# One piece of expert work to each scan, instead of 0.85, beside the last chunk of a Mamba and mixture-of-experts kernel

## The chip, the cores and the metric

The kernel runs on one core of a Trainium2 chip. The metric is device time in microseconds (us) of one execution. Before the change it is 1593.14 us, the median of three runs (1592.46 to 1595.06). The profile comes from one further execution, which took 1591.91 us, with 1590.2 us between its first and its last instruction.

The five engines are named as in the profile: PE (matrix multiply, with its weight loads as PEld), DVE (vector), ACT (activation), POOL (general), SP (issues DMAs). Each runs its own instructions in a fixed order and waits on semaphores for the others.

## The reference, cut to what matters

A layer over 4 sequences of 1024 tokens of 256 channels: a selective-scan (Mamba) block, a layer norm, a mixture of experts with a shared expert, and a second layer norm.

```python
# Mamba block, N = 16 states, 512 inner channels
deltaA  = exp(delta[..., None] * A)
deltaBx = (delta * xs)[..., None] * B[:, :, None, :]
ys      = associative_scan(a*x + b, over time)          # per channel and state
y       = einsum('blcn,bln->blc', ys, C)
x1      = layernorm(x + x + ((y + xs * D) * silu(res)) @ w_out)

# experts: 8, the best 2 of each token, hidden size 1024, and one shared
normed  = rmsnorm(x1)
comb    = top-2 of sigmoid(normed @ router.T), normalised
moe     = shared(normed) + sum over e of comb[:, e] * (relu(normed @ ew1[e] + eb1) @ ew2[e] + eb2)
out     = layernorm(x1 + moe)
```

## The kernel before, in words

The 4096 tokens are cut into 8 chunks of 512, two to a sequence, handled in order. I number them 0 to 7; `chunks[-1]` is chunk 7.

**The scans.** For each chunk the main loop (L1084 on) goes over the 16 states n, and in each over the KB = 4 blocks of 128 channels: 64 scans to a chunk. One scan is an exponential on ACT (`da`, L513) and a scan on DVE (`hs`, L516), 1.21 to 1.27 us each. Once per state DVE also makes the next state's inputs (`hs` from `xs`, L444) and multiplies by C (L529), and POOL adds to `y` (L530). The rows B and C that these take are spread over the partitions by a small matmul on PE (`pb`, L430), issued some scans ahead; its PSUM tiles share a pool of three with other tiles.

**What is put beside the scans.** The work around the scans is written as Python generators, which the main loop steps: `front` (projections, convolution, softplus of the next chunk), `tail` (output projection, layer norm, router and dispatch of the chunk before), and `moe` (the experts). Beside chunk 7 there is no `front`, as no chunk follows; the tail of chunk 6 is stepped once per scan there, through the list `ending`.

**The experts' work.** `moe()` (L975) works through 100 units of 128 token rows: for each chunk 4 units of the shared expert, whose rows are ready when the tail has made `x1T` and `combT`, and then 3, 9, 8, 8, 8, 8, 8 and 16 units of routed rows, which are gathered once the tail has scattered its rows to DRAM (`scatter`, L701) and made its plan. A unit is `up` (32 matmul records, two halves, `pu`, L900; then ReLU on ACT into `h`, L909) and `down` (16 records, two halves, `pd`, L929). Each half ends in a `yield`, so a unit is **four pieces**. The weights of a routed unit, 1 MB for up and 1 MB for down, are fetched per unit on SP's queue into two buffers each. A routed unit ends with an accumulating indirect DMA on POOL (L962); two shared units together end with an accumulating DMA on POOL (L950) out of the single buffer `rs`, which ACT fills (L945).

**How many pieces.** `other_work(share)` (L1079) adds `at_once * share` to an account, `at_once` being 0.85 and the share 1 for these chunks, and takes one piece from `moe` for each whole unit in it. If nothing is ready, `moe` yields False and the account is set to zero. After the last scan the loop `while ending` steps the tail of chunk 7, with one piece after each of its steps; what is left of `moe` follows, and then `finish` reads the sums back, normalises and writes out.

The order in which the code emits work is a priority, not the engines' order: the builder may bring an instruction forward on its engine if its inputs are thought to be ready earlier.

Of the kernel before, what the change touches and what calls it, by code (L numbers as in the profile page):

```python
# [24 lines left out]
LEN, FIRST = {}, {}  # L25
# [3 lines left out]
MAXC = max(LEN.values())  # L29
# [41 lines left out]
def mamba_moe_kernel(  # L71
# [32 lines left out]
    def load_x(b, c):  # L104
        first, n = FIRST[b, c], LEN[b, c]
        t = two.tile([P, n // P, D], F32, tag="x", name=f"x_{b}_{c}", bufs=3)
        nc.sync.dma_start(t, x[b, first : first + n, :].rearrange("(t p) d -> p t d", p=P))
        return t
# [142 lines left out]
    chunks = list(LEN)  # L251
# [173 lines left out]
    def over_partitions(step, row):  # L425

        b, c, n = step
        TC = LEN[b, c]
        pb = ps_mix.tile([P, TC], F32, tag="mix", name=f"pb_{b}_{c}_{row}")
        nc.tensor.matmul(  # L430
            pb, lhsT=pick[:, row : row + 1].to_broadcast([P, P]), rhs=scans[b, c][3],
            start=True, stop=True,
        )
        return pb

    def inputs(step, pb):
        b, c, n = step
        xs, TC = scans[b, c][0], LEN[b, c]

        on_pool = KB - 2 if (b, c) == chunks[0] else KB - 1  # L440
        copy = two.tile([P, TC], F32, tag="b", name=f"b_{b}_{c}_{n}")
        nc.scalar.copy(copy, pb)  # L442
        hs = wide.tile([P, KB, TC], F32, tag="s", name=f"hs_{b}_{c}_{n}")
        nc.vector.tensor_tensor(  # L444
            hs[:, 0:on_pool, :], xs[:, 0:on_pool, :],
            pb.unsqueeze(1).to_broadcast([P, on_pool, TC]), ALU.mult,
        )
        for k in range(on_pool, KB):
            nc.gpsimd.tensor_tensor(hs[:, k, :], xs[:, k, :], copy, ALU.mult)  # L449
        return hs  # L450
# [26 lines left out]
    def diagonal(step):  # L477

        n, TT = step[2], LEN[chunks[0]] // P
        d = two.tile([P, TT, P], F32, tag="w1", name=f"diagonal_{n}")  # L480
        shape = [P, TT, P]
        nc.gpsimd.tensor_tensor(
            d, ident.unsqueeze(1).to_broadcast(shape),
            by_token[1][:, :, n : n + 1].to_broadcast(shape), ALU.mult,
        )
        return d

    def products(step, d):

        n, TT = step[2], LEN[chunks[0]] // P  # L490
        for k in range(KB):
            pool, tag = (ps_dn, "dn") if (n * KB + k) % 3 == 2 else (ps_up, "up")
            pu = pool.tile([P, TT, P], F32, tag=tag, name=f"in_{n}_{k}")
            for t in range(TT):
                nc.tensor.matmul(
                    pu[:, t, :], lhsT=by_token[0][:, t, k * P : (k + 1) * P], rhs=d[:, t, :],
                    start=True, stop=True,
                )
            scaled_inputs.append(pu.rearrange("p t j -> p (t j)"))
            yield  # L500

    def by_pe(step):
        return step[0:2] == chunks[0] and step[2] >= 3

    def scan(step, hs, of):
        b, c, n = step
        delta, TC = scans[b, c][1], LEN[b, c]
        for k in of:
            if by_pe(step):
                da = hid.tile([P, TC], F32, tag="h", name=f"da_{b}_{c}_{n}_{k}")  # L510
            else:
                da = ps_da.tile([P, TC], F32, tag="da", name=f"da_{b}_{c}_{n}_{k}")
            nc.scalar.activation(  # L513
                da, delta[:, k, :], AF.Exp, scale=chan_sb[:, k, CA + n : CA + n + 1]
            )
            nc.vector.tensor_tensor_scan(  # L516
                hs[:, k, :], da, scaled_inputs.pop(0) if by_pe(step) else hs[:, k, :], 0.0 if c == 0 else state[:, k, n : n + 1],
                ALU.mult, ALU.add,
            )

    def keep(step, hs):
        b, c, n = step
        if c + 1 < len(CHUNKS[b]):
            nc.scalar.copy(state[:, :, n : n + 1], hs[:, :, LEN[b, c] - 1 : LEN[b, c]])

    def outputs(step, hs, pb):
        b, c, n = step
        y = scans[b, c][2]
        nc.vector.tensor_tensor(hs, hs, pb.unsqueeze(1).to_broadcast([P, KB, LEN[b, c]]), ALU.mult)  # L529
        nc.gpsimd.tensor_tensor(y, y, hs, ALU.add)  # L530
# [524 lines left out]
    order = [(b, c, n) for b, c in chunks for n in range(N)]  # L1055

    beside, ending, work = [], [], moe()
    at_once = 0.85

    def advance(count):  # L1060
        for _ in range(count):
            if not next(work, False):
                return False
        return True

    def side(of):
        for g in list(of):
            if next(g, "end") == "end":
                of.remove(g)
# [3 lines left out]
    def other_work(share):  # L1073
        nonlocal owed
        owed += at_once * share
        while owed >= 1.0:
            owed = owed - 1.0 if advance(1) else 0.0
# [10 lines left out]
    for i, step in enumerate(order):  # L1088
        b, c, n = step
        place = chunks.index((b, c))  # L1090
        more = i + 1 < len(order)
        for k in range(KB):
            if k == 0 and more and n + 1 < N:
                if by_pe(order[i + 1]):
                    over_b = diagonal(order[i + 1])
                else:
                    over_b = over_partitions(order[i + 1], n + 1)
            if k == KB // 2 and more and by_pe(order[i + 1]):
                coming = products(order[i + 1], over_b)
            next(coming, None)  # L1100
            if k == KB // 2:
                over_c = over_partitions(step, N + n)
                if more and n + 1 == N:
                    over_b = over_partitions(order[i + 1], 0)
            scan(step, hs, [k])
            if k == 0 and late is not None:
                keep(*late[0:2])
            if k == KB // 2 - 1:
                if late is not None:
                    outputs(*late)  # L1110
                    if n == 0:
                        list_of = ending if place + 1 == len(chunks) else beside
                        list_of.append(tail(*chunks[place - 1]))
                if n == 0 and place + 1 < len(chunks):
                    beside.append(front(*chunks[place + 1]))
                if n == 3:
                    beside.append(scans[b, c][4]())
                if n == N // 2 and place + 2 < len(chunks):
                    xs_in[chunks[place + 2]] = load_x(*chunks[place + 2])
                side(beside)  # L1120
            if k == KB - 1:
                late = (step, hs, over_c)
                if more and by_pe(order[i + 1]):
                    hs = wide.tile([P, KB, LEN[b, c]], F32, tag="s", name=f"hs_{b}_{c}_{n + 1}")
                elif more:
                    hs = inputs(order[i + 1], over_b)
                side(beside)
            side(ending)
            other_work(LEN[b, c] / MAXC)
    keep(*late[0:2])  # L1130
    outputs(*late)
    ending.append(tail(*chunks[-1]))
# [73 lines left out]
```

## Time and profile before

| what | value |
|---|---|
| median of three runs | 1593.14 us |
| profiled execution | 1591.91 us, span 1590.2 us |
| chunk 7's scans, first start to last end | 1201.5 to 1358.7 us |
| last sum into `y` of chunk 7 ends (POOL) | 1366.0 us |
| output projection of chunk 7 (`po`) starts on PE | 1366.79 us |
| router of chunk 7 (`pr`) starts on PE | 1392.51 us |
| first routed rows of chunk 7 are transposed on PE | 1423.68 us |
| last expert matmul ends | about 1551 us |
| reading the sums back, layer norm, output | from 1556 us to the end |

Busy time over the span is 1279.8 us on DVE, 1254.7 on PE, 1141.6 on POOL and 1065.6 on ACT. All times in the profile count from the first instruction. A row of a group gives the line in the code, the engine, the operation, the tiles written and read, and the busy time; a row of waits gives who waited for whom, for how long in total, how often, and the longest.

### The profile page before, as it was taken

How to read it: one execution, taken by the hardware profiler on the slowest of the kernel's cores; microseconds unless marked ns; L12 is line 12 of the kernel's file. 1: busy time of each engine (PE TensorE's matmuls, PEld its weight loads, DVE VectorE, ACT ScalarE, POOL GpSimd, SP SyncE). 2: the span in 40 equal slices, each digit the busy share in tenths (PEclk: the TensorE clock that was granted, in tenths of full speed). 3: DMA queues.
4: the chain of work that ended last, by engine and by line, in shares of the span. 5: the costliest groups of instructions: out<-in, count | busy, mean ns of one | idle time of the engine just before them, and what ended most of it. 6: DMA issues, size and time to landing. Idle time of an engine off the chain costs nothing. (4 is left out here: it accounts for less than half of the span.)

```text
span 1590.2 us, 20804 instructions
## 1 busy us (share of the span) xinstructions
PE 1254.7 (79%) x6639; PEld 970.3 (61%) x6639; DVE 1279.8 (80%) x1422; ACT 1065.6 (67%) x2345; POOL 1141.6 (72%) x886
## 2 busy tenths in 40 slices
PE   5588467865688788879798889888879889899990
PEld 2356324652356666677567756776667768789990
DVE  3999899989997898999998999899989899320005
ACT  5757458764778578877788778766886666434442
POOL 2468975798578876998789978997699887431223
PEclk8699678987788999999999999899899999999995
DMA  4000000440016562475236633563166538659996
GB/s 121 1 0 1 26 14 17 146 119 17 13 61 192 173 182 64 147 220 168 50 124 204 190 80 122 159 197 107 35 209 185 153 116 249 177 153 323 315 273 217
DMA packets 160275, 211.64 MB, mean 133 GB/s; under 512 B 20617, under 2 KB 138130, under 8 KB 160162
## 3 DMA queue, kind: packets, MB, share of 16 engines
q1 hardware_dynamic: 135954, 181.75, 35.2%
q0 software_dynamic: 17216, 21.57, 7.6%
q10 hardware_dynamic: 6992, 6.95, 1.3%
q8 instruction: 54, 0.88, 0.2%
q14 instruction: 59, 0.48, 0.1%
HBM read 178.97 MB, written 31.27 MB: 132 GB/s over the span
## 5 line engine op out<-in xcount | busy, mean ns | idle before, releaser
L530 POOL TENSOR_TENSOR y<-y,hs 128x2048 f32<-128x2048 f32 x128 | 597.1, 4665 | 81.2 <-DVE hs L529 80.8
L513 ACT ACTIVATE da<-delta,chan_sb 128x512 f32<-128x512 f32 x512 | 353.0, 697 | 193.1 <-DVE hs L516 190.6
L929 PE MATMUL pd<-w,h 128*128 128x256 f32 x1600 | 386.7, 386 | 22.5 <-ACT h L909 11.5
L929 PEld LDWEIGHTS pd<-w,h 128*128 128x128 f32 x1600 | 298.8, 193 | 92.8 <-issue 20.5
L516 DVE TENSOR_TENSOR_SCAN hs<-da,state,hs 128x512 f32<-128x512 f32 x256 | 317.8, 1270 | 27.1 <-ACT da L513 26.0
L900 PEld LDWEIGHTS pu<-xT,w 128*128 128x128 f32 x2176 | 276.6, 204 | 64.7 <-ACT xT L883 45.5
L900 PE MATMUL pu<-xT,w 128*128 128x128 f32 x2176 | 281.3, 288 | 28.0 <-ACT xT L883 28.0
L529 DVE TENSOR_TENSOR hs<-hs,pb 128x2048 f32<-128x2048 f32 x128 | 290.7, 2271 | 3.3 <-PE pb L430 1.6
L909 ACT ACTIVATE h<-pu,wb 128x128 f32<-128x128 f32 x800 | 229.3, 368 | 71.9 <-PE pu L900 67.2
L516 DVE TENSOR_TENSOR_SCAN hs<-da,hs 128x512 f32<-128x512 f32 x204 | 240.9, 1209 | 21.2 <-ACT da L513 20.7
L449 POOL TENSOR_TENSOR hs<-xs,b 128x512 f32<-128x512 f32 x118 | 170.6, 1448 | 67.9 <-ACT b L442 48.9
L444 DVE TENSOR_TENSOR hs<-xs,pb 128x1536 f32<-128x1536 f32 (+1 forms) x115 | 197.9, 1722 | 13.2 <-ACT b L442 7.5
L962 POOL DMA_INDIRECT sums<-rb,xb x68 | 108.0, 1588 | 131.3 <-ACT xT L883 43.8
L293 PE MATMUL pi<-hT,w_in_sb 128*128 128x512 f32 x256 | 143.0, 683 | 32.6 <-DVE xs L325 12.3
L430 PE MATMUL pb<-parts,pick 128*128 128x512 bf16 x243 | 98.2, 407 | 77.1 <-DVE hs L529 27.6
L900 PEld LDWEIGHTS pu<-x1T,w 128*128 128x128 f32 x1024 | 130.9, 203 | 13.8 <-issue 10.0
L900 PE MATMUL pu<-x1T,w 128*128 128x128 f32 x1024 | 136.4, 290 | 0.0
L219 DVE BATCH_NORM_STATS2 bnst_l<-o 128x6 f32<-128x256 f32 x32 | 11.9, 411 | 153.9 <-DMA o<-sums 153.9
L293 PEld LDWEIGHTS pi<-hT,w_in_sb 128*128 128x128 f32 x256 | 49.9, 213 | 97.3 <-issue 34.2
L562 PE MATMUL po<-w_out_sb,y 128*128 128x256 f32 x256 | 70.0, 435 | 36.6 <-POOL y L552 29.1
L562 PEld LDWEIGHTS po<-w_out_sb,y 128*128 128x128 f32 x256 | 55.5, 222 | 56.3 <-POOL y L552 36.3
L705 POOL DMA_INDIRECT rows<-hn,to x64 | 63.4, 990 | 32.1 <-issue 15.8
(198 smaller groups left out, 1555.8 us busy)
## 6 DMA issues: line engine op xcount, KB each, us to landing
w<-in_ew SPq DMA_DIRECT2D x136, 1024.0 KB, 5.7
w<-in_sw SPq DMA_DIRECT2D x16, 1024.0 KB, 5.3
xb<-rows SPq DMA_DIRECT2D x68, 129.0 KB, 5.1
x<-in_x SPq DMA_DIRECT2D x8, 512.0 KB, 4.2
sums<-summed ACTq DMA_DIRECT2D x8, 512.0 KB, 3.0
sums<-rs POOLq DMA_DIRECT2D x16, 256.0 KB, 6.6
o<-sums SPq DMA_DIRECT2D x3, 1024.0 KB, 8.8
out<-o ACTq DMA_DIRECT2D x3, 640.0 KB, 3.3
```

The lines of the kernel that those rows point to most:

```text
L293: nc.tensor.matmul(pi, lhsT=w_in_sb[:, k, m * P : (m + 1) * P], rhs=hT[:, k, :], start=(k == 0), stop=(k == KD - 1),)
L444: nc.vector.tensor_tensor(hs[:, 0:on_pool, :], xs[:, 0:on_pool, :], pb.unsqueeze(1).to_broadcast([P, on_pool, TC]), ALU.mult,)
L449: nc.gpsimd.tensor_tensor(hs[:, k, :], xs[:, k, :], copy, ALU.mult)
L513: nc.scalar.activation(da, delta[:, k, :], AF.Exp, scale=chan_sb[:, k, CA + n : CA + n + 1])
L516: nc.vector.tensor_tensor_scan(hs[:, k, :], da, scaled_inputs.pop(0) if by_pe(step) else hs[:, k, :], 0.0 if c == 0 else state[:, k, n : n ...
L529: nc.vector.tensor_tensor(hs, hs, pb.unsqueeze(1).to_broadcast([P, KB, LEN[b, c]]), ALU.mult)
L530: nc.gpsimd.tensor_tensor(y, y, hs, ALU.add)
L562: ins = nc.tensor.matmul(po[:, i, :], lhsT=y[:, k, t * P : (t + 1) * P], rhs=w_out_sb[:, k, :], start=(k == 0), stop=(k == KB - 1),)
L900: nc.tensor.matmul(pu[:, i, :], lhsT=w[:, k, at : at + P], rhs=xT[:, k, :], start=(k == 0), stop=(k == KD - 1),)
L909: nc.scalar.activation(t[:, i, :], pu[:, i, :], AF.Relu, bias=wb[:, m : m + 1])
L929: nc.tensor.matmul(pd, lhsT=hidden[h][:, i, :], rhs=w[:, m, :], start=(m == 0), stop=(m == HB - 1 and e is None),)
L962: nc.gpsimd.indirect_dma_start(sums_of[:, :], bass.IndirectOffsetOnAxis(xb[:, TOKEN : TOKEN + 1].bitcast(U32), 0), rb, None, compute_op=AL ...
```

## The change: a share of 1 / 0.85 beside chunk 7

For all chunks but the last, `other_work` gets the same share as before. For the last one the share is divided by `at_once`, so that the account grows by exactly 1.0 with each scan.

```diff
     for i, step in enumerate(order):
         b, c, n = step
         place = chunks.index((b, c))
-        more = i + 1 < len(order)
+        more, more_chunks = i + 1 < len(order), place + 1 < len(chunks)
...
             side(ending)
-            other_work(LEN[b, c] / MAXC)
+
+            other_work(LEN[b, c] / MAXC * (1.0 if more_chunks else 1 / at_once))
```

Nothing is computed that was not computed before, and nothing is left out.

## The prediction

> **What bounds the kernel now.** I first read the page's slices of the span, then cut the stretch that the change touches into windows, and then asked who waits for whom in it.
>
> ```profile
> PE   5588467865688788879798889888879889899990
> ...
> DVE  3999899989997898999998999899989899320005
> ```
>
> Each digit is a fortieth of the span, 39.8 us. DVE is at 9 almost throughout the scans and falls off at slice 34; from there PE is at 9 until slice 39. So two regimes meet where the change acts: scans bounded by DVE, then experts bounded by PE. Moving PE work forward pays if PE has room beside the last scans, and if something shortens behind them. The windows (columns: busy PE, PEld, DVE, ACT, POOL, granted clock, DMA share, GB/s):
>
> ```profile
> 353.00:522.00 169.00, 118.92 (x526) 80.61 (x525) 154.87 (x162) 119.31 (x246) 133.13 (x97) 0.81 0.26 77
> ...
> 703.00:869.00 166.00, 140.29 (x743) 108.80 (x744) 156.03 (x162) 128.62 (x290) 139.44 (x100) 0.95 0.47 138
> ```
> ```profile
> 1201.50:1244.00 42.50, 37.03 (x209) 31.20 (x208) 42.40 (x39) 27.24 (x67) 39.04 (x35) 0.96 0.68 205
> 1244.00:1283.00 39.00, 36.18 (x199) 29.65 (x198) 30.49 (x41) 28.98 (x59) 29.13 (x19) 0.91 0.35 86
> 1283.00:1361.00 78.00, 66.08 (x415) 56.57 (x414) 74.95 (x67) 50.39 (x127) 63.09 (x33) 0.98 0.69 210
> 1361.00:1375.20 14.20, 9.76 (x39) 7.97 (x38) 4.30 (x10) 1.17 (x5) 5.01 (x2) 0.88 0.36 113
> 1375.20:1421.70 46.50, 46.41 (x320) 42.34 (x318) 10.45 (x43) 22.57 (x66) 20.66 (x39) 1.00 0.58 162
> ```
>
> The first pair are the stages of chunks 2 and 4: 27 and 48 pieces (counted below) beside them, and no difference in length, so pieces do hide. The other five are chunk 7's scans in three parts, the hand-over, and the PE-bound tail. In the scans PE is busy 139.3 of 159.5 us: 20 us of room on paper. Now PE's and DVE's waits between 1201 and 1361 us:
>
> ```profile
> PE pbt L879 <- ACT h L909: 6.0, 4, 2.4
> PE pd L929 <- ACT rs L945: 4.3, 1, 4.3
> PE pb L430 <- DVE hs L529: 2.9, 4, 0.9
> ...
> PE pb L430 <- DVE hs L444: 2.1, 4, 0.7
> ```
> ```profile
> DVE hs L516 <- ACT da L513: 5.8, 3, 2.7
> DVE hs L444 <- ACT b L442: 3.9, 2, 3.6
> ```
>
> Only where PE waits for DVE (2.9 + 2.1 = 5.0 us, all in the third part) is it early. The other rows are latency that more pieces do not fill. DVE's own 9.7 us of waits are all behind ACT. One shows how: at 1308.19 ACT's copy into `rs` waited 2.9 us for the earlier sum from `rs` to land, PE stood 4.3 us, its next up half ran slow, the ReLUs waited 4.4 us for it, an exponential stood behind them, and DVE lost 2.4 us at 1314.22. PE being late reaches DVE through ACT's fixed order.
>
> After the scans, PE's timeline:
>
> ```profile
> 1366.79 8.76 PE L562 MATMUL po<-w_out_sb,y 128*128 128x256 f32 x32 [4.44 <-DVE y L550]
> ...
> 1390.35 0.60 PE L227 MATMUL pt_n<-ident,hn 128*128 128x128 f32 x4
> 1390.79 1.89 PE L929 MATMUL pd<-w,h 128*128 128x256 f32 x8
> 1392.51 1.85 PE L617 MATMUL pr<-router_sb,x1T 128*128 128x8 f32 x16
> ...
> 1423.68 0.41 PE L879 MATMUL pbt<-ident,xb 128*128 128x128 f32 x2 [2.04 <-DMA xb<-rows]
> ```
>
> PE stands 4.4 us until `y` is done, then is full, and at 1423.68 waits 2.0 us for the first routed rows. So the path behind the scans is the dispatch (norm, transposes, router, scatters, gather), which just outlasts the PE work beside it.
>
> **The change part by part.**
>
> *How many pieces move.* Before, 64 x 0.85 gives 54 calls. The 21 pieces left of chunk 5 last until scan 24; the shared units of chunk 6 become ready when its tail, stepped once per scan whatever the rate, reaches `combT` at scan 26 (counting from 0). From there 38 scans x 0.85 = 32 pieces. Sum 53. At rate 1 the same 21 pieces are gone at scan 20, five calls find nothing, and 38 follow: 59. So **6 pieces move, not 10**. By the same count, chunks 1 to 7 take 27, 27, 53, 48, 48, 48, 53 = 304 of 320 pieces before; 16 are left for the 19 tail steps until chunk 7's own units are ready, after the change 10.
>
> *What a piece costs.* An up half is 16 records, 1.95 us of PE (row at 1384.36), a down half 8 records, 1.89 us. Six: 3 x 1.95 + 3 x 1.89 = 11.5 us. ACT gets 3 x 1.14 us of ReLU with them. DMA: 6 x 0.5 MB = 3 MB into 78 us, 39 GB/s on top of 210; the tail moves 290, so it fits. POOL's and SP's issues move with the pieces, one or two of each.
>
> *Scans 0 to 26* (first two windows). By scan 26 the same 21 pieces are done. In the first window 2.6 pieces (5 us) come earlier, into a PE that is full: 37.0 us busy and 5.4 waiting of 42.5. In the second they are missing, where DVE idles 8.5 us, 6.3 of it (3.6 for `b`, 2.7 for `da`) behind PE. Both ends: +4 if the lag reaches DVE and the gap gives nothing back, -4 if the gap takes away two thirds of the 6.3. I take 0.
>
> *Scans 26 to 63* (third window). 11.5 us are added. 5.0 take the place of PE's waits for DVE. PE may also end late: 4.4 us of standing before `po` lie behind; of lag DVE notices nothing for about two scans (two `da` tiles, 2 x 1.27 us), say 3.0 with the `pb` that run ahead. 11.5 - 5.0 - 3.0 = **+3.5 us**. Ends: 0, if all lag fits the 4.4 us and the waits; 13.2, if nothing is absorbed and the `rs` wait grows by the 1.7 us by which four pieces get shorter (0.7 scan x 2.45 us).
>
> Here a rule weighs differently: the Trainium skill, "Perfetto Trace Analysis", section Identifying the Most-Contended Engine, says that busy matmul time is a poor measure of PE's headroom, as matmuls are pipelined, and that weight-load busy time is the better one. The row has PE at 85% but PEld at 56.6 of 78, 73%, against 90 to 94% in the PE-bound tail: room for 13 to 17 us, and a stretch of 0. I stay with the waits: PE's gaps lie between waits in a fixed order, and average room is not room at the place where `pb` is due.
>
> *Behind the scans.* PE has 11.5 us less to do, but the dispatch sets the end. Of it PE holds up the second transposes (at 1390.35, though the first were through at 1387.0) and so the router: 3.1 us. A sum of an expert (L962, 1403.47, 1.55 us) sits before the scatter on POOL; sometimes it will be gone: 1.0. Together 4.1. Against this stands a rule of the skill's "TensorE: Matmul & The Clock Gate", Why this matters for your kernels: no PE gaps over some 3 us, else it runs at half clock for a window of 3.4 us. This trace agrees: after the 4.4 us gap the 32 `po` records took 8.76 us, against 2 x 3.62 for the same ones of chunk 6 in stride. Of the 11 pieces that PE runs behind `po` before, 5 stay (9.6 us), for the 14 us from 1375.2 to `x1T` at about 1389: a new gap of 4.5 us just ahead of transposes and router. The router at half clock took 3.54 us beside the scans, against 1.85: 1.7 lost. By the row alone -4.1, by the rule **-2.4**, which I take. Ends: -0.5 (the transposes alone) and -6.7 (all of PE's lead, were the rows in time).
>
> *Behind 1421.7* nothing changes: 16 routed units at 7.25 us, PE-bound, DMA at 0.94.
>
> *Sum:* 0 + 3.5 - 2.4 = +1.1 us on the profiled 1591.9: 1593.0. The median lay 1.2 above that execution: **1594.2 us**.
>
> **The rivals.** *Hidden:* the third part takes the pieces without stretching (for it: 27 or 48 pieces made no difference to chunks 2 and 4; PEld). Then -2 from the gap at scans 21 to 25 and -4.1 behind: about 1587. Against it: DVE is at 75.0 of 78 us, and PE without idle that is its own.
> *PE and ACT become the bound* (slower): one mechanism, in scans 26 to 63. PE's lag passes the two `da` tiles' 2.5 us, exponentials stand behind ReLUs in ACT's order, and DVE runs at PE's pace: 11.5 + 1.7 - 5.0 = 8.2, less 2.4: +5.8, 1599. For it: the chain at 1308, and the stage of chunk 3, 181 us with 53 pieces, against 166 for chunk 5 with 48 and the same 160 us of DVE. Against it: DVE waits were 2.4 us in this part. It decides once more than half the added work finds no wait to replace.
> *The change does little*, since work runs dry: that is the 6 of 10, in the forecast.
>
> **How the numbers follow.** About the same, 0.45, own range 1591 to 1598; hidden 0.25; PE and ACT bound 0.30. What can be told from no change is 0.2%, 3.2 us. Hidden counts as faster; the bound mostly as slower; the middle case spills a little into slower: 0.25, 0.41, 0.34. The range takes in hidden's 1587.5 and the slower case up to +9: 1587.5 to 1602.
>
> **What would show it.** Right: 59 pieces before the last scan; the scans of chunk 7 some 3.5 us longer, the `pb` waits on DVE gone, the `rs` wait over 4.3; a new PE gap near the transposes; router to last scan 3 us closer; the wait for `xb` rows above 2 us. Wrong: scans unchanged in length (then hidden), or DVE waiting for `da` over 10 us (then the bound); or a tail shorter by over 5 us, since then PE and not the dispatch was its limit.

## The result, and the profile after

The changed kernel takes 1600.58 us (median of 8 runs, 1597.72 to 1603.21) against 1593.31 of the kernel before on the same chip: a ratio of 1.0059, 95% interval [1.0039, 1.0078]. By that ratio it is **slower by 9.4 us** (6.2 to 12.4); the two medians lie 7.3 us apart. The profiled execution took 1602.52 us, with a span of 1600.8, 10.6 more than before. Cut by stage, in us (`ahead` is the tile in which DVE compares chunk 6's routing scores):

| stage | before | after |
|---|---|---|
| chunk 7's first scan starts at | 1201.5 | 1199.1 |
| from there to chunk 6's router comparison (L634) on DVE | 63.1 | 75.4 |
| from the comparison to the end of the scans | 94.1 | 91.9 |
| last scan to chunk 7's router (`pr`) | 33.8 | 35.2 |
| last scan to the first routed rows on PE | 64.9 | 66.3 |
| first routed rows to the end of the span | 166.5 | 168.0 |

So of the 10.6 us the scans gave +10.1 (157.2 to 167.3), the hand-over +1.4, what follows +1.5, and the stages before chunk 7's first scan, which the change does not touch, -2.4. The comparison does not stand at one place among the scans: 25 of them lie ahead of it before and 27 after, and two scans are 2.5 us of DVE's work. So I also count by scans. From the start of scan 0 to the start of scan 32, half of them, it takes 85.8 us before and 96.2 after, and from there to their end 71.5 and 71.1: all of the loss is in the first half. The length of the scans repeats within a microsecond: three other kernels with the old rate before scan 28 (`before_store_free`, `tail_first`, `late_only`) have 157.5, 157.6 and 157.9, and a second profile of the changed kernel has 166.6.

The slices of the page of the changed kernel (each digit is a fortieth of the span) hardly show it:

```profile
DVE  4999899989997898899998999899989689320005
```

Before the drop to 3 at slice 34, DVE's row has a lone 6, and that is the place: slice 31, counted from 0, 1241 to 1281 us. The windows of the changed kernel, cut at the same stages as those of before, show it better (columns: the window, its length, busy PE, PEld, DVE, ACT, POOL, granted clock, DMA share, GB/s):

```profile
1199.00:1241.50 42.50, 37.31 (x218) 31.66 (x217) 39.96 (x37) 24.11 (x62) 37.30 (x25) 1.00 0.71 212
1241.50:1279.50 38.00, 27.06 (x142) 21.73 (x143) 25.68 (x23) 23.94 (x52) 24.83 (x20) 0.91 0.31 80
1279.50:1366.50 87.00, 78.88 (x476) 67.42 (x476) 80.74 (x86) 58.80 (x144) 67.56 (x41) 0.94 0.64 202
```

In the second window every engine is idle for a third of the time: PE 27.1 of 38 (36.2 of 39 before), DVE 25.7 (30.5 before), with DMA at 0.31. No engine bounds it. Something stands there. The third window is PE's dense one, and there DVE does its work in 80.7 of 87 us.

Who waits for whom on DVE in all of chunk 7's scans, changed kernel, 1199.1 to 1366.4 us (waiter, releaser, us in total, times, longest):

```profile
DVE ahead L634 <- ACT pr L628: 6.2, 1, 6.2
DVE hs L516 <- ACT da L513: 4.7, 1, 4.7
DVE hs L444 <- POOL y L530: 3.5, 2, 1.7
DVE hs L444 <- ACT b L442: 3.4, 2, 2.3
DVE row L689 <- PE pr L685: 2.3, 1, 2.3
```

and before, 1201.5 to 1358.7 us:

```profile
DVE hs L516 <- ACT da L513: 5.8, 3, 2.7
DVE hs L444 <- ACT b L442: 3.9, 2, 3.6
...
DVE ahead L634 <- ACT pr L628: 0.6, 1, 0.6
```

DVE's idle time in the scans grew by 9.4 us (from 11.6 to 21.0), which is nearly all that they lost. Two long single waits for ACT are new, 6.2 and 4.7 us. In the totals only the first adds: the comparison (`ahead`) waits 5.6 us more, while the one wait of 4.7 for `da` stands in place of three that sum to 5.8. The rest of the growth is 3.5 us of waits for POOL's `y` sums, which were none before, and 1.7 for `row` (from 0.6). The two waits for `y` come at 1310.8 and 1316.6 us, after POOL issued the eight scatters of chunk 6 (1289.5 to 1301.8); no run tested that link.

What ACT waits for is in the timeline. First the changed kernel, taken from the timelines of POOL, ACT and DVE (start, duration, engine, line, operation; in brackets the idle time before it and what ended it):

```profile
1233.67 0.19 POOL L579 TENSOR_SCALAR var<-mv 128x4 f32<-128x4 f32 x1
1233.95 4.51 POOL L530 TENSOR_TENSOR y<-y,hs 128x2048 f32<-128x2048 f32 x1
1238.55 0.19 POOL L580 TENSOR_SCALAR var<-var 128x4 f32<-128x4 f32 x1
...
1244.46 1.09 ACT L243 ACTIVATE hn<-summed,shift_n,root_l 128x256 f32<-128x256 f32 x2 [6.41 <-POOL shift_n L240]
1248.13 2.46 DVE L516 TENSOR_TENSOR_SCAN hs<-da,state,hs 128x512 f32<-128x512 f32 x2 [4.67 <-ACT da L513]
...
1264.14 1.60 POOL L962 DMA_INDIRECT sums<-rb,xb  x1 [0.16 <-issue]
1266.57 0.20 ACT L627 ACTIVATE probs<-pr 128x32 f32<-128x32 f32 x1
1269.95 1.57 POOL L962 DMA_INDIRECT sums<-rb,xb  x1 [2.89 <-issue]
1273.84 0.37 ACTq L624 DMA_DIRECT2D sums<-summed  x1
1274.25 0.18 ACT L628 ACTIVATE pr<-pr 128x32 f32<-128x32 f32 x1 [7.48 <-DMA sums<-rb,xb]
1274.46 0.42 DVE L634 TENSOR_TENSOR ahead<-pr,probs 128x256 f32<-128x256 f32 x1 [6.23 <-ACT pr L628]
```

**The norm stand.** Chunk 6's layer norm is a chain of 0.2 us operations on POOL. Between its first (L579) and its second (L580) POOL's order now has a `y` sum of 4.51 us. ACT, next in its own order with `hn`, stands 6.4 us, the exponential stands behind `hn`, and DVE loses 4.7. **The store stand.** ACT also issues the DMA that stores chunk 6's rows into `sums` (L624). It goes out only at 1273.84, after both accumulating sums (L962) of chunk 5's last two units, though these add to other rows. The second sigmoid (L628) reads the same tile as the first (L627, 1266.57), but comes behind the store in ACT's order: ACT stands 7.5 us on a DMA issue, and DVE 6.2. Before the change (its POOL and ACT timelines) the norm's chain ran ahead of the `y` sum, and the store was out between the sums:

```profile
1232.48 0.19 POOL L579 TENSOR_SCALAR var<-mv 128x4 f32<-128x4 f32 x1 [1.18 <-DVE mv L220]
1232.76 0.19 POOL L580 TENSOR_SCALAR var<-var 128x4 f32<-128x4 f32 x1
...
1238.81 0.60 ACT L243 ACTIVATE hn<-summed,shift_n,root_l 128x256 f32<-128x256 f32 x1 [1.15 <-POOL shift_n L240]
1238.88 4.54 POOL L530 TENSOR_TENSOR y<-y,hs 128x2048 f32<-128x2048 f32 x1
...
1251.17 1.61 POOL L962 DMA_INDIRECT sums<-rb,xb  x1 [0.17 <-issue]
1258.44 0.37 ACTq L624 DMA_DIRECT2D sums<-summed  x1
1267.69 1.57 POOL L962 DMA_INDIRECT sums<-rb,xb  x1 [0.16 <-issue]
1273.35 1.58 POOL L962 DMA_INDIRECT sums<-rb,xb  x1 [2.77 <-ACT rb L959]
```

For the store the cause is in the order of emission, which the order in the two traces bears out. At 0.85 the last sums of chunk 5 were emitted after the tail's store. At 1.0 the 21 pieces are used up before it, so both sums are emitted ahead of it, and `sums` being one tensor to the builder, the store is made to wait for them.

PE's waits after, 1200 to 1375 us and then 1368 to 1562 us, for the lines that the prediction read:

```profile
PE pu L900 <- ACT xT L883: 7.4, 3, 5.2
...
PE pb L430 <- ACT res L306: 5.5, 1, 5.5
...
PE pb L430 <- DVE hs L529: 0.4, 1, 0.4
```
```profile
PE po L562 <- DVE y L550: 5.6, 1, 5.6
PE pbt L879 <- DMA xb<-rows: 5.0, 1, 5.0
```

The waits for DVE before `pb` are gone (5.0 to 0.4). In their place PE stands 5.2 us once for `xT` and 5.5 once for `res`, copies that sit behind the two stands in ACT's order: 1245.45 us is the first `xT` after the norm stand. PE's first records behind that gap are also slow, 3.58 us for a half of `up` that takes 1.95 in stride:

```profile
1245.85 3.58 PE L900 MATMUL pu<-xT,w 128*128 128x128 f32 x16 [5.16 <-ACT xT L883]
```

And behind the scans PE stands longer for `y` (5.6) and for the first routed rows (5.0 against 2.0): it has less to do in a hand-over that did not get shorter.

### The profile page after: what moved, and what is told of

It reads as the page before. It is cut to its first block, busy times and chain, and to the rows that moved or that the text cites. A ratio compares the mean times of both kernels' runs of the same rounds, so it can differ in the third digit from the quotient of the medians.

```text
span 1600.8 us, 20808 instructions
## 1 busy us (share of the span) xinstructions
PE 1252.7 (78%) x6633; PEld 966.4 (60%) x6639; DVE 1280.0 (80%) x1422; ACT 1065.2 (67%) x2345; POOL 1141.7 (71%) x886
## 5 line engine op out<-in xcount | busy, mean ns | idle before, releaser
L929 PE MATMUL pd<-w,h 128*128 128x256 f32 x1600 | 391.6, 389 | 18.8 <-ACT h L909 11.3
L900 PE MATMUL pu<-xT,w 128*128 128x128 f32 x2176 | 278.9, 286 | 35.5 <-ACT xT L883 35.4
L962 POOL DMA_INDIRECT sums<-rb,xb x68 | 108.5, 1596 | 138.0 <-issue 44.4
L293 PE MATMUL pi<-hT,w_in_sb 128*128 128x512 f32 x256 | 143.3, 686 | 32.1 <-DVE xs L325 11.6
L900 PEld LDWEIGHTS pu<-x1T,w 128*128 128x128 f32 x1024 | 129.9, 202 | 14.3 <-issue 11.6
L293 PEld LDWEIGHTS pi<-hT,w_in_sb 128*128 128x128 f32 x256 | 49.9, 214 | 97.8 <-issue 35.6
```

What stands on the lines that cost most here:

```text
L293: nc.tensor.matmul(pi, lhsT=w_in_sb[:, k, m * P : (m + 1) * P], rhs=hT[:, k, :], start=(k == 0), stop=(k == KD - 1),)
L900: nc.tensor.matmul(pu[:, i, :], lhsT=w[:, k, at : at + P], rhs=xT[:, k, :], start=(k == 0), stop=(k == KD - 1),)
L929: nc.tensor.matmul(pd, lhsT=hidden[h][:, i, :], rhs=w[:, m, :], start=(m == 0), stop=(m == HB - 1 and e is None),)
L962: nc.gpsimd.indirect_dma_start(sums_of[:, :], bass.IndirectOffsetOnAxis(xb[:, TOKEN : TOKEN + 1].bitcast(U32), 0), rb, None, compute_op=AL ...
```

## The experiments

The theories at the outset:

- **A**: the time is lost in scans 0 to 26 by stands that come of the order of sums, store and norm.
- **B**, the slower rival of the prediction: PE's lag passes through ACT to DVE in scans 26 to 63.

Later ones, for the hand-over and for the first part:

- **C**: the dispatch sets the end, and pieces ahead of it hold it up.
- **D**: the amount of work left on PE sets the end.
- **E**: the first part is long because PE has too many pieces in it.
- **F**: what counts at the hand-over is the priority of the pieces left.

Scans 0 to 27 are states n below 7. "Scans" is their length, 157.2 us before and 167.3 after; "comparison" is the stretch from the first scan to the comparison (63.1 and 75.4); "router" and "rows" are when PE starts on the router and takes the first routed rows, counted from the last scan (33.8 and 64.9; 35.2 and 66.3).

### The change again, and its two halves

`after_again` is the changed kernel unaltered.

> The changed kernel once more, on the same chip as the others: 1.006 of before by both theories.

1.0063 [1.0040, 1.0086], scans 166.6, comparison 75.3. The result stands, and so does its place.

The halves, each on the kernel before:

```diff
-            other_work(LEN[b, c] / MAXC)
+            other_work(LEN[b, c] / MAXC * (1 / at_once if not more_chunks and n >= 7 else 1.0))   # late_only
+            other_work(LEN[b, c] / MAXC * (1 / at_once if not more_chunks and n < 7 else 1.0))    # early_only
```

> Rate 1 only from state 7 of chunk 7 on (scan 28), 0.85 before it: the six added pieces of the third part stay, the early exhaustion of chunk 5's pieces goes. Theory A (the early part: with chunk 5's pieces used up by scan 20, the sums of its last two units are ordered before chunk 6's store into the sums, and ACT stands in front of that store): chunk 7's scans take about 157 us as before, no wait of ACT near the store, and the time is that of before within 3 us. Theory B (the rival of the prediction: PE's lag in scans 26 to 63 reaches DVE through ACT): scans about 165 us, time about 1600.

> Rate 1 only in states 0 to 6 of chunk 7, 0.85 from state 7 on. Theory A: the store still waits for the last sum of chunk 5, ACT stands 5 to 8 us, chunk 7's scans about 164 us, time about 1599. Theory B: scans about 157 us, time about 1593 as before.

`late_only`: 1.0026 [1.0012, 1.0040], scans 157.9, router 37.1, rows 68.8. `early_only`: 1.0083 [1.0059, 1.0108], scans 169.9, comparison 75.2, rows 64.1. The faster rate in scans 28 to 63, where B has its mechanism, leaves the scans nearly as they were (+0.6), so **B falls**. The faster rate in scans 0 to 27 alone makes the 64 scans 12.6 us longer, 7.3 of it by the start of scan 32. A second execution of `late_only`, under the label `late_tail_first`, took 1594.16 us and has the same stages (157.9, 37.2, 70.0).

The halves do not add up to the whole: 0.26% and 0.83% against 0.59%. One reason is visible in the second half of `early_only`'s scans (ACT's waits, 1200 to 1371 us): the copy into `rs`, the single buffer, stands 7.8 us, against 2.9 before and 0.8 after the whole change.

```profile
ACT rs L945 <- DMA sums<-rs: 7.8, 1, 7.8
ACT pr L628 <- DMA sums<-rb,xb: 7.3, 1, 7.3
ACT hn L243 <- POOL shift_n L240: 6.4, 1, 6.4
```

The two others are the stands of A. A second `rs` buffer was not tried, so its share stays open.

### The store set free

The sums of earlier chunks and the store of this one touch different rows, so the store need not wait. The edit tells the builder so; on the kernel after (`after_store_free`) and before (`before_store_free`):

```diff
+    added = []
...
-        nc.scalar.dma_start(own_sums.rearrange("(t p) d -> p t d", p=P), summed)
+        ins = nc.scalar.dma_start(own_sums.rearrange("(t p) d -> p t d", p=P), summed).ins
+        for other in added:
+            tc.declare_no_dep(ins, other, reason="rows of earlier chunks")
...
-            nc.gpsimd.indirect_dma_start(
+            added.append(nc.gpsimd.indirect_dma_start(
...
-            )
+            ).ins)
```

> The changed kernel, but the store of a chunk's rows into the sums no longer waits for the accumulating sums of earlier chunks' units (their rows are disjoint). Theory A: ACT's 7.5 us stand is gone, DVE's 6.2 us behind it too, scans about 161 us (what is left is the 4.7 us behind the layer norm's chain on POOL), time about 1594 to 1596. Theory B: no change against the changed kernel, 1600.

> The kernel before, with the same freed store (control). Theory A: before, the store beside chunk 7 waited for nothing late, so the scans stay at 157 us; in the tail of chunk 7 ACT stood up to 5 us in front of the same store, which may give 0 to 3 us: 1590 to 1593. Theory B: 1593.

After: scans 167.3 to 161.8, comparison 75.4 to 69.0, with 27 scans ahead of it in both. Before: scans 157.5, unchanged, and 1.0006 [0.9993, 1.0019], as nothing stands there. ACT's timeline of `after_store_free` (its lines are one to three higher):

```profile
1263.81 0.37 ACTq L625 DMA_DIRECT2D sums<-summed  x1
...
1266.27 0.19 ACT L631 ACTIVATE pr<-pr 128x32 f32<-128x32 f32 x1
```

The store goes out some 10 us earlier and the sigmoid follows without a wait. So **5.6 us of the 10.1 in the scans are the store stand** (4.8 against the second profile of the changed kernel). In what is left, +4.5, DVE's waits for POOL's `y` sums are the ones that grew: 6.1 us in two, where `before` has none. Why POOL is late there no run singled out. The time of the whole fell to 1.0044 [1.0029, 1.0058], an interval that overlaps 1.0059's; that the end gains all of it is not shown.

### The norm stand: an attempt that missed

To take the norm chain out of POOL's order, chunk 6's was put on DVE, alone, with the free store, and on the kernel before with the free store (`before_both_freed`):

```diff
+        by = nc.vector if (b, c) == chunks[-2] else nc.gpsimd
...
-        nc.gpsimd.tensor_tensor(shift, mean, scale, ALU.mult)
+        by.tensor_tensor(shift, mean, scale, ALU.mult)
```

and so for the other small operations of the chain.

> The changed kernel, with the small operations of chunk 6's layer norm (from the variance to the shift, 18 of them) on DVE instead of POOL, so that no sum into y of 4.5 us can be ordered between them. Theory A (two stands of ACT in the early part: before hn for POOL's chain, before the store for the sums): the first goes, 4.7 us of DVE's wait, against some 3 us of added DVE work; the store's stand stays: scans about 165 us instead of 167, ratio about 1.005. Theory E (the early part is long because PE is full there, whatever waits are shown): no change, 1.006.

> The changed kernel with the freed store and the layer norm's chain on DVE, both. Theory A: both stands gone, chunk 7's scans about 159 us, the router's comparison about 65 us behind the first scan (75 after the change, 63 before), ratio about 1.002, the rest being the hand-over. Theory E: as with the freed store alone, scans 162, ratio 1.0044.

> The kernel before with the same two edits (control, and a candidate to beat both). Theory A: neither stand was there before; the chain on DVE costs up to 3 us: ratio 1.000 to 1.002. Theory E: the same.

1.0064 [1.0041, 1.0087], 1.0039 [1.0025, 1.0052] and 1.0057 [1.0034, 1.0081]; scans 168.5, 163.1 and 167.6. The third decides: on the kernel before, which has no such stand, the edit alone costs 10 us of scans. So none of the three says what the stand on POOL costs. Where the 10 us go is in the traces of `before_both_freed`, here DVE's and POOL's:

```profile
1229.10 3.36 DVE L582 TENSOR_SCALAR var<-var 128x4 f32<-128x4 f32 x1
```
```profile
1227.92 4.52 POOL L531 TENSOR_TENSOR y<-y,hs 128x2048 f32<-128x2048 f32 x1
```

A DVE operation on 128x4 values took 3.36 us and ended 0.03 us behind POOL's `y` sum, which had begun before it. Two others of the chain took 3.51 and 3.49 us and ended as closely behind a `y` sum; a fourth took 0.79 and ended so behind a shorter operation of POOL. The other 16 took 0.13 to 0.17 us, so the four account for 10.5 us. The same shows in `after_norm_on_dve` (3.51 and 1.20). What couples the two engines no run here shows.

### One stand at a time, by the rate

The rate can put the pieces so that only one stand arises. `first4_only` has rate 1 for states 0 to 3 and catches up down to the old count; `mid_only` hurries in states 4 to 6 alone.

```diff
+... (1.0 if n < 4 else 0.6 if n < 7 else at_once) / at_once    # first4_only
+... (1.5 if 4 <= n < 7 else at_once) / at_once                 # mid_only
```

> Rate 1 in states 0 to 3 of chunk 7, 0.6 in states 4 to 6, 0.85 after: the store keeps its place ahead of the last two sums, and the first four states have 16 pieces instead of 13. Theory A: ACT stands about 6 us at hn, none at the store; comparison about 67 us behind the first scan, scans about 161 us, ratio about 1.003. Theory E: PE is full in the first four states, so these get longer by up to 3 x 1.9 us, without one long stand; scans about 161 as well: told apart by the waits.

> Rate 0.85 in states 0 to 3 of chunk 7 as before, 1.5 in states 4 to 6, 0.85 after: chunk 5's pieces are used up at scan 20 as after the change, so the last sums come ahead of the store, but the first four states, beside which the layer norm's chain runs, are as before. Theory A (stands from the order of sums and store): ACT stands 5 to 8 us at the store, none at hn; comparison about 69 us behind the first scan, scans about 163 us, ratio about 1.004. Theory E (the number of pieces early on): the same 21 pieces by the router as before, scans 157, ratio 1.000.

`first4_only`, waits on ACT and on DVE in the first part:

```profile
ACT hn L243 <- POOL shift_n L240: 6.4, 1, 6.4
```
```profile
DVE hs L516 <- ACT da L513: 4.7, 1, 4.7
```

`mid_only`, ACT's waits:

```profile
ACT pr L628 <- DMA sums<-rb,xb: 5.7, 1, 5.7
...
ACT hn L243 <- POOL shift_n L240: 1.1, 1, 1.1
```

The waits part cleanly. `first4_only` has the norm stand to the digit and no store stand: scans 158.5 (+1.3), 1.0029 [1.0016, 1.0041]. `mid_only` has the store stand (5.7 of the 7.5 us) and almost nothing of the norm stand: scans 159.5 (+2.2), 1.0025 [1.0012, 1.0039]. Each edit alone makes the kernel slower. The prices do not part as cleanly. At the comparison (66.2 and 68.8) they can't be read, since 24 scans lie ahead of it in `first4_only` and 28 in `mid_only`. By scans, this is how much later than before the nth starts behind scan 0 (in us, the last column for the end of the scans):

| kernel | n = 20 | 24 | 28 | 32 | end |
|---|---|---|---|---|---|
| before, the time itself | 46.8 | 61.3 | 72.9 | 85.8 | 157.2 |
| after | +7.6 | +1.8 | +7.7 | +10.4 | +10.1 |
| after_store_free | +7.6 | +1.8 | +1.3 | +2.3 | +4.5 |
| first4_only | +7.7 | +7.0 | +9.9 | +4.4 | +1.3 |
| mid_only | 0.0 | -4.7 | -1.4 | +4.1 | +2.2 |
| slow_early_only (below) | +1.5 | -1.4 | -5.7 | -7.1 | -7.0 |

The norm stand puts scan 20 7.6 us late. In the changed kernel most of that is back by scan 24: before, DVE waited 3.6 us for `b` there (at 1258.9), and after the change it does not; other work of DVE also shifts past such a mark. The store stand is what sets `after` apart from `after_store_free` from scan 28 on. In both edits here the pieces move too (rates of 0.6 and 1.5 in states 4 to 6), and fewer pieces save time by themselves, as the next experiment shows. So neither +1.3 nor +2.2 is the price of a stand alone: the store stand has its 5.6 us from the freed store, and how the other 4.5 of the 10.1 divide between the norm stand and the waits for `y` stays open.

### Fewer pieces in the first part

If 1.0 is too much there, is 0.85 too? `slow_early` takes 0.75 below n = 7 and then 1.0; `slow_early_only` takes 0.75 and then the old 0.85.

```diff
+... (0.75 if n < 7 else 1.0) / at_once        # slow_early
+... (0.75 if n < 7 else at_once) / at_once    # slow_early_only
```

> Beside chunk 7 a rate of 0.75 in states 0 to 6 and 1 from state 7 on. Theory A: the early part only gets dearer when chunk 5's pieces run out ahead of the tail's store; slower than 0.85 changes nothing there: comparison 62 to 64 us behind the first scan, ratio 1.000 to 1.003 as with rate 1 late alone. Theory E: the early part gets shorter with fewer pieces, comparison about 58 us behind the first scan, ratio below 1.

> Rate 0.75 in states 0 to 6 of chunk 7 and 0.85 after, so that 18 pieces are left in the code behind the last scan, enough for the 19 steps of the tail as before (16), instead of 12 with rate 1 later. Theory F (what moves is priority: pieces that the code has given out ahead of the dispatch's steps go ahead of them on PE): scans about 153 us as with the slow early part and rate 1 later, but rows about 65 us behind the last scan as before, not 71: ratio 0.997 to 0.998. Against it (the time saved in the scans comes back behind them whatever the order): rows about 69, ratio 1.000.

Comparison 57.1 in both, against 63.1; scans 152.9 and 150.2. Totals 0.9992 [0.9977, 1.0007] and **0.9965 [0.9951, 0.9980]**, 1586.41 us against 1591.05: the second beats both kernels. DVE's waits of `slow_early_only` over all of its scans, 1198 to 1349 us:

```profile
DVE hs L444 <- POOL y L530: 3.6, 4, 1.7
DVE hs L516 <- ACT da L513: 0.3, 1, 0.3
```

The waits for `b` are gone, and of those for `da` 0.3 us is left. So E has a part too: 0.85 was already more than the first part can take, for a reason other than the two stands, as in the kernel before ACT's wait for `hn` was 1.2 us, and none for the store. In the first part ACT now waits 2.6 us for the output of a down (`rb`) against 6.4 before, and no longer for the router's product (3.0 before), which fits a PE that is less full. Whether that is the whole reason, or the order of other instructions again, no run parts.

### The hand-over

`tail_first` is the kernel before with no pieces between the steps of chunk 7's tail; `late_then_tail_first` is the same on `late_only`.

```diff
     while ending:
         side(ending)
-        advance(1)
```

> The kernel before, but behind the last scan the tail of chunk 7 is emitted whole, with no piece between its steps; the leftover pieces follow in the code and come behind it in priority. Theory C (the dispatch of chunk 7 sets the end, and pieces emitted ahead of its steps hold it up on PE, however few they are): router about 31 us behind the last scan instead of 33.8, rows about 61 instead of 64.9, time 3 to 4 us shorter, 0.998. Theory D (PE's amount of work sets the end): no gain, 0 to 4 us longer, as PE may stand in front of the router.

> Rate 1 from state 7 of chunk 7 on, and the tail of chunk 7 emitted whole behind the last scan. Theory C: the late added pieces cost the hand-over only through their priority; with the tail first, router about 31 us behind the last scan against 37.1 with pieces between, time equal to or below before. Theory D: as with rate 1 late alone, 1.0026.

The router comes at 29.2 and 28.8 us, so pieces do hold it up, by 4.6 us. Neither kernel gains: 1.0244 [1.0216, 1.0272] and 1.0053 [1.0030, 1.0075]. The first is far outside what C and D expected of it, the second above both. PE's timeline of `tail_first`, then SP's, then SP's waits from 1355 to 1425 us:

```profile
1419.13 0.69 PE L879 MATMUL pbt<-ident,xb 128*128 128x128 f32 x2 [21.71 <-DMA xb<-rows]
```
```profile
1398.79 8.44 SPq L722 DMA_DIRECT2D rows<-empty  x8
...
1416.07 0.35 SPq L856 DMA_DIRECT2D xb<-rows  x1
```
```profile
SPq L721 <- DVE to L699: 40.7, 1, 40.7
SPq L856 <- DMA rows<-hn,to: 6.1, 1, 6.1
```

PE has work of chunk 6 left, but the loads of its rows (L856) are now emitted behind chunk 7's tail on SP's queue. There SP stands 40.7 us for the tail's `to` (L721), needs 8.4 for the writes of L722, and the first load waits another 6.1 for the tail's scatters, which write the same DRAM tensor. So PE stands 21.7 us. The pieces between the tail's steps are what brings those loads out earlier. `late_then_tail_first` has less of chunk 6 left and is spared this (166 us from the rows to the end, as before, against 206 in `tail_first`), but PE takes the rows at 72.4, without a wait for them. An early router is not an early start on the rows.

What the pieces in between cost depends on when they were emitted. On PE the router waits for eight transposes (`pt_n`, L227). PE's timeline after, then `slow_early_only`:

```profile
1392.50 3.62 PE L929 MATMUL pd<-w,h 128*128 128x256 f32 x16
1396.69 3.72 PE L929 MATMUL pd<-w,h 128*128 128x256 f32 x16 [0.56 <-ACT rb L959]
1400.24 1.04 PE L227 MATMUL pt_n<-ident,hn 128*128 128x128 f32 x8
```
```profile
1376.77 0.60 PE L227 MATMUL pt_n<-ident,hn 128*128 128x128 f32 x4
...
1380.72 0.60 PE L227 MATMUL pt_n<-ident,hn 128*128 128x128 f32 x4
```

After the change all eight come behind two whole downs; in `slow_early_only`, as before, the first four slip in early. The number of chunk 6's pieces left after the last scan, as the code emits them and as PE's records have them (records of `pu` and `pd` after the last scan less chunk 7's own, over 16 and 8), beside the router and the rows:

| kernel | left in the code | left on PE | router | rows |
|---|---|---|---|---|
| mid_only | 15 | 11.5 | 32.4 | 66.3 |
| early_only | 16 | 13.9 | 32.4 | 64.1 |
| before | 16 | 13.0 | 33.8 | 64.9 |
| first4_only | 17 | 13.4 | 35.5 | 69.6 |
| slow_early_only | 18 | 14.4 | 35.6 | 66.3 |
| after | 10 | 10.25 | 35.2 | 66.3 |
| late_only | 11 | 12.3 | 37.1 | 68.8 |
| slow_early | 12 | 12.9 | 38.7 | 71.3 |

`before` and `slow_early` leave the same work on PE, and their rows are 6.4 us apart; `slow_early_only` leaves more than `slow_early`, and its rows come 5.0 earlier. So the amount on PE alone does not set it (**D falls** as it was put). In `first4_only` and `slow_early_only` PE takes the rows without a wait, so there its own work comes last; in the other six it waits for them, 2.0 to 5.6 us. Where PE has run ahead of the code by two pieces or more (first five rows) the router comes at 32.4 to 35.6; where it has not (last three), at 35.2 to 38.7: pieces emitted during the scans and still undone go ahead of the tail's transposes. C and F fit this, with some overlap between the groups (the rows of `first4_only` come at 69.6); no run changed the priority alone.

## Why the prediction was wrong, point by point

*Pieces that move.* Right by a count of the code (53 pieces to 59, 6 moved; 10 were left of 16). On PE it was 2.75 (13.0 to 10.25), since before the change PE had already run three pieces ahead of the code. The step counted calls, and costed the path behind the scans by them.

*Scans 0 to 26: "I take 0", ends -4 and +4.* **This is the step that failed.** By the start of scan 27 it measured +8.6 us, and +10.4 by scan 32, near the end of its two windows. (At the start of scan 26 the changed kernel was even 1.6 us early; the store stand comes right behind that scan.) The step bounded only PE's lag, and the sentence "POOL's and SP's issues move with the pieces, one or two of each" was left without a price. The two sums on POOL that moved ahead of the store are the store stand; in the norm stand POOL's `y` sum got in between two operations of a chain, `first4_only` showing that the early pieces bring that about. The store stand was worth 5.6 us; the rest of the 10.1 is not divided. PE's waits could not show either, and neither could the waits of before, in which the store passed without one.

*Scans 26 to 63: +3.5.* The late half of the rate alone added 0.6 us to the scans, and in the changed kernel the part from scan 32 on is 0.3 shorter. The `pb` waits went as expected. The `rs` wait, which was to pass 4.3 us on PE, is no longer among PE's waits there, and its source on ACT shrank from 2.9 to 0.8. The reading by PEld, room of 13 to 17 us and a stretch of 0, was nearer here than the one by waits that I took.

*Behind the scans: -2.4.* It measured +1.4 to the rows and +1.5 behind them. The direction of the piece count was right; the assumption that fewer pieces behind the last scan let transposes and router through sooner was wrong: the second transposes no longer came late behind the first, all eight came late. The gap at half clock, which the clock-gate rule was weighed for, did not come there: the only idle time that PE had near the transposes was 0.56 us. It came in the scans instead, behind the norm stand (3.58 us for 1.95). And of chunk 6's 32 `po` records the step read only the second 16, in stride, at 3.62 us; the first 16, behind a gap of 2.11, took 5.41, so here a gap below the 3 us of the rule was followed by slow records as well. The wait for the rows above 2 us came (5.0).

*The rivals.* 1599 for "PE and ACT become the bound" is near the time that came, but its place and mechanism are not: with rate 1 in its part alone (`late_only`), the scans stay. It was near by luck. "Hidden" was right for scans 26 to 63 and wrong for the rest.

*The sum.* 0 + 3.5 - 2.4 = +1.1 was to be read as (10.1 in all the scans) + 1.4 + 1.5, less 2.4 that the stages before it differed between the two executions.

## What to carry to other kernels

When filler work moves earlier, list every queue instruction that moves with it (sums, stores, gathers) and ask for each which later instruction is now emitted behind it, touches the same tensor and sits in a compute engine's own in-order queue: its wait costs that engine everything behind it. A rate that is right on average can be wrong in one stage: here a faster rate in scans 28 to 63 left the scans nearly alone (+0.6 us), in scans 0 to 27 it made them 12.6 us longer, and a slower one there was the gain (0.9965). When two kernels are compared up to a mark, check that the same work lies ahead of it: here the comparison stood behind 24 to 28 scans. Count the work left at a hand-over on the engine, not in the code, and look at what was emitted before it: here downs that were overdue went ahead of the transposes.

## What was not expected of the hardware

A DMA whose issue takes 0.37 us on ACT held ACT for 7.5 us when what it waited for was late, and DVE for 6.2. A POOL operation of 4.51 us between two of 0.2 us cost ACT 6.4 us and DVE 4.7 by the same route. And moving 18 operations on 128x4 and 128x8 values from POOL to DVE, each some 0.2 us on POOL, cost 10 us of scans (157.5 to 167.6): four of them ended only when an operation of POOL did, three of these after 3.36 to 3.51 us.
